# A graph layer without its column copies: VectorE's four copies a step go, GpSimd gathers eleven more times

## The chip, the cores and the metric

One Trainium2 chip, one NeuronCore of it. The kernel is one launch. The metric is device time in microseconds (us); lower is better. A core has five engines with queues of their own: TensorE (PE, matrix products into PSUM), VectorE (DVE), ScalarE (ACT), GpSimd (POOL) and SyncE (SP, here only a queue that issues DMAs). Transfers can be issued from SP, ACT and POOL.

## The reference

A message-passing layer over 12,500 nodes with 64 features and 200,000 edges that are sorted by destination. For every edge a gate is computed from its own 64 features and its distance, and a hidden state from its two end nodes; their product is added up at the destination, and a small network and a layer norm finish each node:

```python
nodes = node_state[edges].reshape(num_edges, -1)          # x[src], x[dst]
gates = ssp(edge_state @ We1 + be1) @ We2 + be2
gates = gates * (1.0 - sigmoid(5.0 * (edges_distance - 3.5)))
h = ssp(nodes @ Wn1 + bn1) @ Wn2 + bn2
message_sum = zeros.at[edges[:, 1]].add(h * gates)
new_state = node_state + (ssp(message_sum @ Ws1 + bs1) @ Ws2 + bs2)
out = layernorm(x + new_state)                            # ssp(x) = softplus(x) - log 2
```

Destinations are sorted, so their rows can be read as a window of a table. Sources are random: the 64 numbers of each of 200,000 source nodes have to be fetched one by one.

## The kernel before

**Groups and steps.** The edges are cut into 391 groups of 512, and a group into four slots k = 0 to 3 of 128 edges, one edge to a partition. The main loop (line 694) has one step i for each group. In the order in which each engine gets its instructions, step i does this:

- PE: `transposes(i+1)` (lines 346 to 356) turns the four slots of group i+1 from edges by features to features by edges; two bias products; `scatter(i-1)` (line 433), which adds the messages of group i-1 up by destination; `layer1_edge(i+1)` (line 370), `layer1_node(i+1)` (line 377), and the second layer of group i, `layer2` (lines 411 and 416).
- ACT: `xcopy(i+1)` (line 360) takes the transposed sources out of PSUM, then `exps` and `logs` (lines 391 and 394) make the softplus.
- DVE: `window(i-1)` (line 450) adds the scattered sums into the table of sums; `columns(i)` (lines 316 to 334); then `hcut(i)` (line 425), which waits for `layer2(i)` of PE, `message(i)` (line 429), `softplus(i+1)` (line 399) and `onehot(i+3)` (line 339).

A step of the loop closes through several engines: `hcut` lets `message` start, `message` lets PE's `scatter` start, `softplus` and `onehot` come before `window` on DVE, and PE's `layer1_edge` waits for `window`. In this document a step is counted from one `hcut` to the next.

**How a source row comes in.** There are three ways, and a slot is given to one of them beforehand:

1. Gathers. `gather(g)` (lines 245 to 257) issues one indirect DMA for a slot from POOL's queue: 128 rows of 256 bytes. The tiles of 18 groups (`AHEAD + BEHIND`) exist. The loop emits `gather(i+14)` in step i, but on POOL's own queue nothing holds it back except a free tile, and a tile is free when the scatter of the group 18 before it is done. So the gathers of group i+18 are issued as one burst right after `scatter(i)`.
2. Rows. Slots in `slots_by_rows` (47 of them) are fetched by plain DMAs of one row each, seven in a step from SP's queue and nine from ACT's (`fetch`, line 273).
3. Columns. Slots in `slots_by_columns` (line 119: slot 1 of the groups 42, 74, 106, ... 362, eleven in all). A copy of x, transposed, with nodes 0 to 6249 on partitions 0 to 63 and the rest on partitions 64 to 127, lies in SBUF as `xh`. In each of the steps 8 to 359 `columns(i)` loads four column numbers into registers of DVE (line 322) and copies four columns, each [128, 1] (line 329). After 32 steps the 128 columns of a slot are there, and one more operation (line 333) sets the half that belongs to the other node to zero. For such a slot no gather is issued, its part of the gather tile is set to zero (line 253), and `layer1_node` adds one more product on PE, `wn1_twice` by the chosen columns (line 380).

**Around the loop.** Before it, POOL issues the gathers of 14 groups back to back, and PE, ACT and DVE make the table of the nodes' own products (line 652) and write it out. `xh` comes in by four DMAs on SP's queue in steps 0 to 3 (line 700); the column numbers and the sides come in by two DMAs on SP's queue (lines 564 and 565), `wn1_twice` by two on ACT's (line 589), and three operations of DVE prepare them (lines 663 to 665). Nodes whose last edge is done go through the final network in blocks of 512, whose parts are spread over the following steps (`node_block`, lines 452 to 537); the last 512 nodes are two blocks of 256.

Of the kernel before, what the change touches and what calls it, by code (L numbers as in the profile page):

```python
# [42 lines left out]
F32 = mybir.dt.float32  # L43
BF16 = mybir.dt.bfloat16
I32 = mybir.dt.int32
U8 = mybir.dt.uint8
AF = mybir.ActivationFunctionType
OP = mybir.AluOpType
# [3 lines left out]
DVE = mybir.EngineType.DVE  # L52
# [5 lines left out]
P = 128  # L58
D = 64
# [6 lines left out]
K = 4  # L66
# [13 lines left out]
COLUMNS = 4  # L80
COLUMNS_FROM = 8
XH_PARTS = 4
# [34 lines left out]


def slots_by_columns(NG):

    slots = []
    for g in range(NG - 2):
        if (g - 3 - COLUMNS_FROM + 1) * COLUMNS >= (len(slots) + 1) * P:
            slots.append((g, 1))
    return slots


def column_columns(NG):

    return -(-len(slots_by_columns(NG)) // COLUMNS) * COLUMNS  # L130

# [8 lines left out]
def gnn_resnorm_kernel(ctx: ExitStack, tc: tile.TileContext, a: dict, out: bass.AP, E: int):  # L140
    nc = tc.nc
    x = a["x"]
    N = x.shape[0]
    NG = a["eT"].shape[1]
# [6 lines left out]
    REST = LOADS + 2  # L151
# [32 lines left out]
    packed, at = {}, 0  # L184
# [16 lines left out]
    half_n = a["xh"].shape[1]  # L201
    by_columns = {slot: n for n, slot in enumerate(slots_by_columns(NG))}
    columns_i = const.tile([P, column_columns(NG)], I32, name="columns_i")
    sides_i = const.tile([P, len(by_columns) * P], I32, name="sides_i")
    sides = sides_i.bitcast(F32)
    sign = const.tile([P, 1], F32, name="sign")
    border = const.tile([P, 1], F32, name="border")
    wn1_twice = const.tile([P, 2 * D], F32, name="wn1_twice")
# [33 lines left out]
    def padding(g, k):  # L242
        return g * GE + k % 2 * HE + k // 2 * P >= E

    def gather(g):

        xg = loads.tile([P, K, P], F32, name="xg", bufs=AHEAD + BEHIND)
        xgs[g] = xg
        for k in range(K):
            if (g, k) in by_rows:  # L250
                continue
            if padding(g, k) or (g, k) in by_columns:
                nc.vector.memset(xg[:, k, :D], 0.0)
                continue
            note(("gather", g), nc.gpsimd.indirect_dma_start(  # L255
                out=xg[:, k, :D], out_offset=None, in_=x,
                in_offset=bass.IndirectOffsetOnAxis(ap=src_i[:, g, k : k + 1], axis=0)))
# [56 lines left out]
    column_tiles, chosen_columns, columns_done = {}, {}, [0]  # L314

    def columns(i, pool):

        n = columns_done[0]
        if i < COLUMNS_FROM or n >= len(by_columns) * P:
            return  # L320
        p, q = (n // COLUMNS) % P, n // (COLUMNS * P) * COLUMNS
        _, at = nc.values_load_multi_w_load_instructions(  # L322
            columns_i[p : p + 1, q : q + COLUMNS], engines=[DVE], min_val=0, max_val=half_n - 1,
            skip_runtime_bounds_check_because="src holds rows of x")
        slot = list(by_columns)[n // P]
        if n % P == 0:
            column_tiles[slot] = pool.tile([P, P], F32, name="column", bufs=2)
        for j in range(COLUMNS):
            nc.vector.tensor_copy(column_tiles[slot][:, n % P + j : n % P + j + 1], xh[:, bass.ds(at[j], 1)])  # L329
        columns_done[0] += COLUMNS  # L330
        if columns_done[0] % P == 0:
            chosen_columns[slot] = pool.tile([P, P], F32, name="chosen", bufs=2)
            nc.vector.scalar_tensor_tensor(chosen_columns[slot], sides[:, n // P * P : (n // P + 1) * P], border,
                                           column_tiles[slot], OP.is_ge, OP.mult)

# [37 lines left out]
    def layer1_node(g):  # L373
        for h in range(2):
            zn = zs[g][:, h, HE * (1 - h) : HE * (2 - h)]
            chosen = [t for t in range(2) if (g, 2 * t + h) in by_columns]
            nc.tensor.matmul(zn, wns[:, g % REST, h, :], xTs[g][:, h], start=True, stop=not chosen,  # L377
                             skip_group_check=True)
            for t in chosen:
                nc.tensor.matmul(zn[:, t * P : (t + 1) * P], wn1_twice, chosen_columns[g, 2 * t + h], start=False,  # L380
                                 stop=True, skip_group_check=True)
# [162 lines left out]
    with tc.manual_schedule():  # L544
# [4 lines left out]
        with tc.tile_pool(name="prep", bufs=1) as prep:  # L549
# [14 lines left out]
            nc.sync.dma_start(columns_i, a["columns"])  # L564
            nc.sync.dma_start(sides_i, a["sides"].partition_broadcast(P))
# [21 lines left out]

            for h in range(2):
                nc.scalar.dma_start(wn1_twice[h * D : (h + 1) * D, :], a["Wn1"][:D, :])
                nc.vector.memset(sign[h * D : (h + 1) * D], 2.0 * h - 1.0)  # L590
                nc.vector.memset(border[h * D : (h + 1) * D], float(half_n if h else 1 - half_n))
# [55 lines left out]
            for i in range(PARTS):  # L647
# [10 lines left out]
                if i == 1:  # L658
                    nc.vector.tensor_copy(base_i[:1], base_b[:1])
                    nc.vector.tensor_scalar(base_i[32:33], base_b[32:33], float(8 * D), None, OP.mult)  # L660
                    nc.vector.tensor_scalar(rows_i, rows_i, float(4 * D), None, OP.mult)
                    upper = prep.tile([P, column_columns(NG)], F32, name="upper")
                    nc.vector.tensor_scalar(upper, columns_i, float(half_n), float(-half_n), OP.is_ge, OP.mult)
                    nc.vector.tensor_tensor(columns_i, columns_i, upper, OP.add)
                    nc.vector.tensor_scalar(sides, sides_i, sign, None, OP.mult)
                    for k in range(2):
                        nc.vector.tensor_copy(be3[:, k, :], rows[:, 0, :])
                    for k in range(K):
                        nc.vector.tensor_copy(row3[:, :, k, :], rows[:, 1:3, :])
                        nc.vector.tensor_copy(rs3[:, k, :], rows[:, 3, :])  # L670
# [9 lines left out]
        with tc.tile_pool(name="finish", bufs=1) as finish:  # L680
            xh = finish.tile([P, half_n], F32, name="xh")
# [12 lines left out]
            for i in range(-1, last - 1):  # L694
# [3 lines left out]
                if 0 <= i < XH_PARTS:  # L698
                    part = slice(half_n * i // XH_PARTS, half_n * (i + 1) // XH_PARTS)
                    nc.sync.dma_start(xh[:, part], a["xh"][:, part])  # L700
# [13 lines left out]
                columns(i, finish)  # L714
# [168 lines left out]
def layouts(inputs):  # L883
# [12 lines left out]
    def padded(v, n, fill):  # L896
        return np.concatenate([v, np.full((n - v.shape[0],) + v.shape[1:], fill, v.dtype)])
# [13 lines left out]
    chosen = np.concatenate([out["src_l"].reshape(P, NG, K)[:, g, k] for g, k in slots_by_columns(NG)])  # L911
    out["sides"] = np.ascontiguousarray(chosen)
    v = padded(chosen, P * column_columns(NG), 0).reshape(-1, P, COLUMNS)
    out["columns"] = np.ascontiguousarray(v.transpose(1, 0, 2).reshape(P, -1))
    half_n = -(-N // 2)
    out["xh"] = np.ascontiguousarray(np.concatenate([x[:half_n].T, padded(x[half_n:], half_n, 0.0).T]))
# [45 lines left out]
```

## Time and profile before

| | |
|---|---|
| median of 3 runs | 3303.51 us (3302.15 to 3305.52) |
| the profiled execution | 3302.15 us, with a span of 3300.4 us inside it |
| busy: PE, POOL, DVE, ACT | 2543.6, 1421.1, 1209.9, 968.5 us |
| granted TensorE clock, mean | 0.735 of full speed |
| gathers by POOL (line 255) | 1505, 944 ns each |
| row fetches: SP's queue, ACT's queue | 2688 and 3328 |
| column copies by DVE (line 329) | 1408, 153 ns each |

The first `hcut` is at 152.9 us and the last at 3286.4 us, so the 390 steps between them take 8.03 us each on average.

How such a profile is read: a line of the page's groups gives source line, engine and operation, the tiles it writes and reads, the count, then the busy time and the mean of one instruction, and after the bar the idle time of that engine just before these instructions with what ended most of it. A line of the timeline gives the start, the duration, the engine, the line and the operation; in brackets stands how long the engine was idle before and what ended it. "remote" means that the trace shows nothing that ended the wait. PE products are pipelined and their ends are modelled. The granted clock changes between 0.5 and 1.0 in this trace, and nothing in between.

### The profile page before, as it was taken

How to read it: one execution, taken by the hardware profiler on the slowest of the kernel's cores; microseconds unless marked ns; L12 is line 12 of the kernel's file. 1: busy time of each engine (PE TensorE's matmuls, PEld its weight loads, DVE VectorE, ACT ScalarE, POOL GpSimd, SP SyncE). 2: the span in 40 equal slices, each digit the busy share in tenths (PEclk: the TensorE clock that was granted, in tenths of full speed). 3: DMA queues.
4: the chain of work that ended last, by engine and by line, in shares of the span. 5: the costliest groups of instructions: out<-in, count | busy, mean ns of one | idle time of the engine just before them, and what ended most of it. 6: DMA issues, size and time to landing. Idle time of an engine off the chain costs nothing.

```text
span 3300.4 us, 50822 instructions
## 1 busy us (share of the span) xinstructions
PE 2543.6 (77%) x11400; PEld 2046.8 (62%) x11400; DVE 1209.9 (37%) x4216; ACT 968.5 (29%) x1323; POOL 1421.1 (43%) x1509
## 2 busy tenths in 40 slices
PE   1678788887777787878778877778877778777787
PEld 1566666666666666666666666666666666666565
DVE  1333333333333333333333333333333333333334
ACT  0232322232232232323233332323232233233333
POOL 7144444444444444444444444444444444444410
PEclk9976776676777667776777777777777676777767
DMA  5321111111111111111111111111111111111110
GB/s 144 120 53 39 41 39 39 37 40 38 44 39 40 40 38 43 39 46 38 43 39 40 41 40 43 42 41 41 37 45 41 41 42 41 41 42 41 42 34 14
DMA packets 152151, 147.35 MB, mean 45 GB/s; under 512 B 53023, under 2 KB 99147, under 8 KB 151842
## 3 DMA queue, kind: packets, MB, share of 16 engines
q1 hardware_dynamic: 95498, 92.19, 9.9%
q0 software_dynamic: 48160, 49.41, 7.7%
q10 hardware_dynamic: 8184, 2.44, 0.4%
q8 instruction: 96, 1.57, 0.2%
q14 instruction: 213, 1.74, 0.2%
HBM read 134.23 MB, written 9.63 MB: 44 GB/s over the span
## 4 chain that ended last, share of the span: by engine, by line
PE 59%; DVE 16%; issue 8%; another core or an unknown queue 8%; DVEq 7%; DMA 1%; SPq 0%; POOL 0%; ACT 0%; ACTq 0%; POOLq 0%
PE z L377 16%; PE gh L416 13%; PE z L370 11%; PE gh L411 8%; PE tx L353 5%; DVE h L425 4%; DVEq L441 4%; DVE s L399 4%; PE z L433 3%; DVEq L322 2%; DVE sums L450 2%; DVE xg L339 2%; DVE msg L429 2%; PE z L652 1%
## 5 line engine op out<-in xcount | busy, mean ns | idle before, releaser
L255 POOL DMA_INDIRECT xg<-in_x,src_i x1505 | 1420.9, 944 | 1740.8 <-PE z L433 564.5
L391 ACT ACTIVATE u<-z 128x768 f32<-128x768 f32 x392 | 316.9, 808 | 1706.0 <-issue 962.6
L425 DVE TENSOR_TENSOR h<-gh,cut 128x256 f32<-128x256 f32 x391 | 165.8, 424 | 1749.8 <-PE gh L416 854.3
L370 PE MATMUL z<-eT,consts 128*128 128x256 f32 x782 | 406.9, 617 | 378.3 <-DVE sums L450 309.8
L377 PE MATMUL z<-xT,wns 106*128 106x256 f32 x1564 | 657.7, 567 | 0.2 <-ACT xT L360 0.2
L416 PEld LDWEIGHTS gh<-consts,s 128*128 128x128 f32 x3128 | 540.3, 259 | 0.1
L416 PE MATMUL gh<-consts,s 128*128 128x64 f32 x3128 | 532.1, 330 | 0.0
L377 PEld LDWEIGHTS z<-xT,wns 106*128 106x128 f32 x1564 | 461.7, 295 | 112.0 <-ACT xT L360 0.9
L433 PE MATMUL z<-xg,msg 128*128 128x84 f32 x1556 | 313.2, 332 | 271.5 <-DVE msg L429 262.4
L433 PEld LDWEIGHTS z<-xg,msg 128*128 128x128 f32 x1556 | 245.1, 225 | 430.2 <-DVE msg L429 417.9
L370 PEld LDWEIGHTS z<-eT,consts 128*128 128x128 f32 x782 | 164.8, 263 | 447.2 <-DVE sums L450 371.3
L411 PEld LDWEIGHTS gh<-consts,s 128*128 128x128 f32 x1564 | 378.3, 298 | 56.8 <-DVE s L399 0.7
L394 ACT ACTIVATE u<-u,one 128x768 f32<-128x768 f32 x392 | 365.9, 933 | 69.7 <-issue 52.0
L399 DVE SCALAR_TENSOR_TENSOR s<-u,z 128x768 f32<-128x768 f32 x392 | 368.9, 941 | 10.7 <-ACT u L394 9.8
L411 PE MATMUL gh<-consts,s 128*128 128x128 f32 x1564 | 365.3, 380 | 0.4 <-DVE s L399 0.4
L360 ACT COPY xT<-tx 106x512 f32<-106x512 f32 x391 | 228.4, 584 | 414.0 <-PE tx L353 293.2
L353 PE MATMUL tx<-consts,xg 128*106 128x128 f32 x1517 | 282.2, 315 | 6.4 <-DMA wns<-table 6.4
L353 PEld LDWEIGHTS tx<-consts,xg 128*106 128x106 f32 x1517 | 222.3, 174 | 10.6 <-issue 8.0
L329 DVE COPY column<-xh 128x1 f32 x1408 | 174.2, 153 | 110.5 <-issue 104.7
L450 DVE TENSOR_TENSOR sums<-sums,z 64x42 f32 x778 | 150.7, 194 | 86.6 <-issue 38.2
L429 DVE TENSOR_TENSOR msg<-gh,h 128x256 f32<-128x256 f32 x391 | 165.8, 424 | 13.4
L404 PE MATMUL gh<-row,ones 3*128 3x512 bf16 x391 | 160.6, 411 | 0.0
(110 smaller groups left out, 756.6 us busy)
## 6 DMA issues: line engine op xcount, KB each, us to landing
xr<-in_x ACTq DMA_DIRECT2D x3328, 0.2 KB
eT<-in_eT SPq DMA_DIRECT2D x195, 256.0 KB
xr<-in_x SPq DMA_DIRECT2D x2688, 0.2 KB
xg<-in_x,src_i POOLq DMA_INDIRECT x1505
wns<-table SPq DMA_DIRECT2D x782, 21.0 KB
table<-tb SPq DMA_DIRECT2D x14, 448.0 KB
sums<-in_xT SPq DMA_DIRECT2D x7, 455.0 KB
y<-in_x SPq DMA_DIRECT2D x23, 128.0 KB
```

Of the source, the lines that this page charges most:

```text
L255: note(("gather", g), nc.gpsimd.indirect_dma_start(out=xg[:, k, :D], out_offset=None, in_=x, in_offset=bass.IndirectOffsetOnAxis(ap=src_i[ ...
L353: ins = nc.tensor.transpose(tx[:, k, :], xgs[g][:, k, :DW], ident)
L370: nc.tensor.matmul(zs[g][:, 0, :HE], we1.rearrange("a h d -> a (h d)"), eTs[g], start=False, stop=True, skip_group_check=True)
L377: nc.tensor.matmul(zn, wns[:, g % REST, h, :], xTs[g][:, h], start=True, stop=not chosen, skip_group_check=True)
L391: nc.scalar.activation(us[g][:, part], z_of(g)[:, part], AF.Exp)
L394: nc.scalar.activation(us[g][:, part], us[g][:, part], AF.Ln, bias=one)
L399: nc.vector.scalar_tensor_tensor(ss[g].rearrange("p i t e -> p (i t e)")[:, part], us[g][:, part], BIG, z_of(g)[:, part], OP.min, OP.max)
L411: nc.tensor.matmul(v[:, 0, t], ss[g][:, 0, t, :], we2, start=False, stop=False, skip_group_check=True)
L416: nc.tensor.matmul(ghs[g][:, 1, 2 * t + h, :], ss[g][:, 1 + h, t, :], wn2, start=False, stop=h == 1 and t == 1, skip_group_check=True)
L425: nc.vector.tensor_mul(hs[g], ghs[g][:, 1], cut[:, g, :].to_broadcast([P, K, D]))
L429: nc.vector.tensor_mul(msgs[g], ghs[g][:, 0], hs[g])
L433: ins = nc.tensor.matmul(sc, msgs[g][:, 2 * t : 2 * t + 2, :].rearrange("p h f -> p (h f)"), xgs[g][:, 2 * t : 2 * t + 2, D:DW], start=t = ...
```

## The change

The column copies and all that serves them are taken out: `slots_by_columns`, `columns`, `xh` with its four loads, the two loads of numbers and sides, the two loads of `wn1_twice`, the memsets of `sign` and `border`, the three preparing operations, the extra product of `layer1_node`, and the arrays made for them on the host. The eleven slots that came by columns are gathered by POOL like any other: 1516 gathers in place of 1505, and no zeroing of their tiles. Nothing else moves: rows, loads, node blocks and the order of the loop stay as they are.

```diff
@@ slots
-def slots_by_columns(NG):
-    slots = []
-    for g in range(NG - 2):
-        if (g - 3 - COLUMNS_FROM + 1) * COLUMNS >= (len(slots) + 1) * P:
-            slots.append((g, 1))
-    return slots
@@ gather
-            if padding(g, k) or (g, k) in by_columns:
+            if padding(g, k):
                 nc.vector.memset(xg[:, k, :D], 0.0)
                 continue
@@ columns
-    def columns(i, pool):
...
-        _, at = nc.values_load_multi_w_load_instructions(
-            columns_i[p : p + 1, q : q + COLUMNS], engines=[DVE], min_val=0, max_val=half_n - 1,
...
-        for j in range(COLUMNS):
-            nc.vector.tensor_copy(column_tiles[slot][:, n % P + j : n % P + j + 1], xh[:, bass.ds(at[j], 1)])
...
-            nc.vector.scalar_tensor_tensor(chosen_columns[slot], sides[:, n // P * P : (n // P + 1) * P], border,
-                                           column_tiles[slot], OP.is_ge, OP.mult)
@@ layer1_node
-            chosen = [t for t in range(2) if (g, 2 * t + h) in by_columns]
-            nc.tensor.matmul(zn, wns[:, g % REST, h, :], xTs[g][:, h], start=True, stop=not chosen,
+            nc.tensor.matmul(zn, wns[:, g % REST, h, :], xTs[g][:, h], start=True, stop=True,
                              skip_group_check=True)
-            for t in chosen:
-                nc.tensor.matmul(zn[:, t * P : (t + 1) * P], wn1_twice, chosen_columns[g, 2 * t + h], start=False,
-                                 stop=True, skip_group_check=True)
@@ before the loop
-            nc.sync.dma_start(columns_i, a["columns"])
-            nc.sync.dma_start(sides_i, a["sides"].partition_broadcast(P))
...
-            for h in range(2):
-                nc.scalar.dma_start(wn1_twice[h * D : (h + 1) * D, :], a["Wn1"][:D, :])
-                nc.vector.memset(sign[h * D : (h + 1) * D], 2.0 * h - 1.0)
-                nc.vector.memset(border[h * D : (h + 1) * D], float(half_n if h else 1 - half_n))
...
-                    nc.vector.tensor_scalar(upper, columns_i, float(half_n), float(-half_n), OP.is_ge, OP.mult)
-                    nc.vector.tensor_tensor(columns_i, columns_i, upper, OP.add)
-                    nc.vector.tensor_scalar(sides, sides_i, sign, None, OP.mult)
@@ the loop
-                if 0 <= i < XH_PARTS:
-                    part = slice(half_n * i // XH_PARTS, half_n * (i + 1) // XH_PARTS)
-                    nc.sync.dma_start(xh[:, part], a["xh"][:, part])
...
-                columns(i, finish)
```

More of the change, by code (lines that the diff above doesn't have):

```diff
@@ L79 @@
 LANDED = 4
-COLUMNS = 4
-COLUMNS_FROM = 8
-XH_PARTS = 4
 CUTOFF = 5.0
@@ L116, in slots_by_rows @@
     return slots
-def slots_by_columns(NG):
-    slots = []
-    for g in range(NG - 2):
-        if (g - 3 - COLUMNS_FROM + 1) * COLUMNS >= (len(slots) + 1) * P:
-            slots.append((g, 1))
-    return slots
-def column_columns(NG):
-    return -(-len(slots_by_columns(NG)) // COLUMNS) * COLUMNS
 def row_columns(NG):
@@ L200, in gnn_resnorm_kernel @@
     rs3 = const.tile([PIECES, K, D], BF16, name="rs3")
[L201 to L208, printed above, removed]
     wns = const.tile([DW, REST, 2, 2 * D], F32, name="wns")
@@ L312, in load @@
                 table_bytes[:, bass.ds(bases[g][h], 8 * D * W)].rearrange("o (w f) -> (o w) f", w=W))), old)
-    column_tiles, chosen_columns, columns_done = {}, {}, [0]
-    def columns(i, pool):
[L318 to L321, printed above, removed]
-        _, at = nc.values_load_multi_w_load_instructions(
-            columns_i[p : p + 1, q : q + COLUMNS], engines=[DVE], min_val=0, max_val=half_n - 1,
[L324 to L327, printed above, removed]
-        for j in range(COLUMNS):
[L329 to L332, printed above, removed]
-            nc.vector.scalar_tensor_tensor(chosen_columns[slot], sides[:, n // P * P : (n // P + 1) * P], border,
-                                           column_tiles[slot], OP.is_ge, OP.mult)
     xTs, zs, us, ss, ghs, hs, msgs, scs = ({} for _ in range(8))
@@ L661, in gnn_resnorm_kernel @@
                     nc.vector.tensor_scalar(rows_i, rows_i, float(4 * D), None, OP.mult)
-                    upper = prep.tile([P, column_columns(NG)], F32, name="upper")
-                    nc.vector.tensor_scalar(upper, columns_i, float(half_n), float(-half_n), OP.is_ge, OP.mult)
-                    nc.vector.tensor_tensor(columns_i, columns_i, upper, OP.add)
-                    nc.vector.tensor_scalar(sides, sides_i, sign, None, OP.mult)
                     for k in range(2):
@@ L680, in gnn_resnorm_kernel @@
         with tc.tile_pool(name="finish", bufs=1) as finish:
-            xh = finish.tile([P, half_n], F32, name="xh")
             blocks = list(zip(node_blocks(N), block_steps(N, NG)))
@@ L910, in layouts @@
     out["rows"] = np.ascontiguousarray(np.concatenate(rows, axis=1))
[L911 to L916, printed above, removed]
     out["dst_l"] = lanes(dst, dst[-1])
```

## The prediction

> **What bounds the kernel now.** I read the page's groups first, then the chain of waits, then the timeline of single steps. By the page POOL looks harmless and DVE's copies look free:
>
> ```profile
> span 3300.4 us, 50822 instructions
> L255 POOL DMA_INDIRECT xg<-in_x,src_i x1505 | 1420.9, 944 | 1740.8 <-PE z L433 564.5
> L425 DVE TENSOR_TENSOR h<-gh,cut 128x256 f32<-128x256 f32 x391 | 165.8, 424 | 1749.8 <-PE gh L416 854.3
> L329 DVE COPY column<-xh 128x1 f32 x1408 | 174.2, 153 | 110.5 <-issue 104.7
> ```
>
> POOL is idle for 1740.8 us, waiting for scatters to free tiles, and it works 17 to 18 groups ahead of PE. DVE idles 1749.8 us in front of `hcut` (4.5 us a step), and the copies lie inside that time. The chain names PE's products. The timeline of a step whose PE work ran at full clock tells something else:
>
> ```profile
> 253.95 0.68 PE L433 MATMUL z<-xg,msg 128*128 128x84 f32 x4
> 254.90 0.94 POOL L255 DMA_INDIRECT xg<-in_x,src_i  x1 [3.05 <-PE z L433]
> 255.38 0.50 DVE L329 COPY column<-xh 128x1 f32 x4
> 256.14 0.94 POOL L255 DMA_INDIRECT xg<-in_x,src_i  x1 [0.30 <-issue]
> 257.22 1.00 PE L416 MATMUL gh<-consts,s 128*128 128x64 f32 x8
> 257.39 0.95 POOL L255 DMA_INDIRECT xg<-in_x,src_i  x1 [0.30 <-issue]
> 258.64 0.94 POOL L255 DMA_INDIRECT xg<-in_x,src_i  x1 [0.31 <-issue]
> 260.75 0.42 DVE L425 TENSOR_TENSOR h<-gh,cut 128x256 f32<-128x256 f32 x1 [4.87 <-remote]
> 260.81 0.58 ACT L360 COPY xT<-tx 106x512 f32<-106x512 f32 x1 [1.93 <-remote]
> ```
>
> PE's last product of `layer2` ends at 258.22, but `hcut`, which needs nothing else, starts at 260.75, and ACT's `xcopy` 0.06 us behind it. Both start 1.2 us after the last gather of the burst ended (259.58), which is when its data land: in the packet records of the gather queue the last landing of a burst lies 1.17 to 1.19 us, on average, behind its last gather. Here is a step whose burst has three gathers, because slot 1 of group 202 comes by columns:
>
> ```profile
> 1624.81 0.67 PE L433 MATMUL z<-xg,msg 128*128 128x84 f32 x4 [0.66 <-DVE msg L429]
> 1625.75 0.94 POOL L255 DMA_INDIRECT xg<-in_x,src_i  x1 [3.03 <-DVE s L399]
> 1627.00 0.94 POOL L255 DMA_INDIRECT xg<-in_x,src_i  x1 [0.30 <-issue]
> 1628.08 1.00 PE L416 MATMUL gh<-consts,s 128*128 128x64 f32 x8
> 1628.24 0.94 POOL L255 DMA_INDIRECT xg<-in_x,src_i  x1 [0.30 <-issue]
> 1630.12 0.42 DVE L425 TENSOR_TENSOR h<-gh,cut 128x256 f32<-128x256 f32 x1 [3.39 <-PE tx L353]
> ```
>
> Again `hcut` comes 0.94 us after the last gather, but that one ended 1.25 us sooner, and the step took 6.25 us. After the last gather of all, PE alone decides:
>
> ```profile
> 3237.46 1.00 PE L416 MATMUL gh<-consts,s 128*128 128x64 f32 x8
> 3238.50 0.42 DVE L425 TENSOR_TENSOR h<-gh,cut 128x256 f32<-128x256 f32 x1 [2.94 <-PE gh L416]
> ```
>
> So something that PE signals to DVE and ACT is held until a burst has landed. Why a transfer that is needed 15 steps later holds them, the trace does not show; that it does, it shows all over. I went through steps 0 to 371 by the starts of `hcut`, the scatters and the gathers. A burst starts 0.27 us after its scatter and 1.88 us after `hcut` at the earliest; four gathers take 4.69 us from first start to last end, three 3.44. Of 317 steps with four gathers 255 have the next `hcut` within 1.35 us of the burst's end; of 52 with three only 20. The floor of a step with four gathers is 1.88 + 4.69 + 1.17 = 7.74 us, and 7.7 to 7.8 is the commonest step. Between steps 8 and 359 a step with four gathers takes 8.18 us on average (299), with three 7.45 (49): 0.73 less.
>
> **The change part by part.**
>
> *Eleven more gathers.* Each of the eleven slots sits in a burst of three that becomes one of four: 1.25 us later (0.94 and an issue of 0.30). What the step pays is 1.25 + 1.17 less the distance that `hcut` has now from the burst's end, and nothing where that is over 2.42. In the steps that start at 342.5, 596.9, 853.3, 1112.9, 1369.5, 1623.9, 1880.6, 2140.4, 2404.0, 2667.7 and 2930.2 us the distances are 1.51, 2.21, 2.67, 1.06, 1.45, 0.94, 2.04, 1.94, 3.52, 0.96 and 1.07. The price is 0.91, 0.21, 0, 1.36, 0.97, 1.48, 0.38, 0.48, 0, 1.46 and 1.35: **+8.6 us**. The average gives 11 x 0.73 = 8.0. Ends: 0, if the burst holds nothing, and 11 x 1.25 = 13.8. POOL itself has the time, and the data are needed 15 steps later.
>
> *The product with `wn1_twice` goes* (line 380; 0.43 us in the chain at half clock, so about 0.22 at full). It lies on PE between `layer1_node` and `layer2`, on the way to `hcut`, in eleven steps. In eight of them `hcut` stands 1.01 to 1.26 us behind a burst, so the landing covers it. In the other three (735.1, 2807.1, 3067.3 us) it gives 0.22 to 0.43: **-0.65 us** at the full-clock price of all three, ends 0 and 11 x 0.43 = -4.7.
>
> *The preparation.* DVE's three operations stand in front of the copy that frees PE's buffer: `sides` starts at 107.99, and PE resumes at 110.37.
>
> ```profile
> 107.99 0.95 DVE L665 TENSOR_SCALAR sides_i<-sides_i,sign 128x1408 f32<-128x1408 int32 x1
> 110.37 5.84 PEld L652 LDWEIGHTS z<-consts,sums 65*128 65x128 f32 x27 [1.74 <-DVE tb L655]
> ```
>
> They go from 107.70 to 108.86, and PE's products run one behind the other from there to the end of the table: **-1.15 us**, ends 0 and -1.2. The five small and large loads ahead of that on SP's and ACT's queues (704, 6 and twice 32 KB, and their places among the transfers' semaphores) give nothing: the x parts behind them were in by 43 us, while PE and ACT stood still until 104.3 us in a stretch full of gathers that stay. I keep 10 us either way for that stretch.
>
> *The column work in the loop.* Per step one register load, four address operations and four copies, 0.5 us, start 0.06 us after the sums, and `hcut` waits 4 us more: 0, and the cover is PE's half of the step (5.2 us on average), which at its shortest, 2.94 us at full clock, still covers the 1 us. The zeroing (11 x 0.11 us) and the selection (11 x 0.35) lie in the same shadow. `xh`'s four loads (781 KB) on SP's queue, past the loads and rows of steps 0 to 3: the bursts there land 1.1 us after their end like the others, so 0.
>
> The sum is 8.6 - 0.65 - 1.15 = +6.8 us on the profiled execution's 3302.15, which is 1.4 below the median. On the median: 3303.51 + 6.8 = **3310.3**, said as 3310.5. That is +0.21%, and about 0.2% (6.6 us) is what a measurement of this kernel can tell from no change.
>
> [...] The gathers in the stretch with copies (206 to 3047 us) take 943 ns each, those without (3055 to 3140 us) 943 ns as well, and the last landing of a burst comes 1.17 to 1.19 us behind its end with the copies and 1.17 without. [...]
>
> **The rivals.**
>
> 1. *The copies make the hold longer; faster.* A single mechanism at the end of the burst: with the copies `hcut` stands 1.176 us behind it (mean of 234 landing-bound steps), without them 1.11 (11 steps at both ends of the loop). If the copies are the cause, 255 x 0.066 = 17 us come back: 3310.3 - 17 = 3293. It passes zero at 0.027 us a step and 0.2% faster at 0.053. For it: the steps at 177.9 and 198.4 us, just before the copies start, took 6.33 and 6.23 us at full clock with four gathers, where all 47 like them with copies took 7.66 to 8.0. Against it: the ones at 3051.8 and 3109.8 us, without copies, took 7.78 and 7.70, and the landings themselves are no sooner.
> 2. *POOL's burst is only a bystander*, as its idle time says and as its lead of 17 groups suggests. Then the gathers cost 0 and the rest stands: 3303.5 - 1.8 = 3301.7, no change. Against it: 0.73 us between steps of three and four gathers.
> 3. *The longer bursts cost more than themselves.* While PE waits for a landing its clock falls (0.5 in most of PE's halves, 0.74 overall), and a step that follows may lose its full clock. If each of the eleven pays the whole 1.25 us and the step behind it the 0.44 us by which the average (8.18) stands over the floor (7.74), it is 11 x 1.69 - 1.8 = +16.8 us: 3320. Against it: the step after one with three gathers takes 8.17 us now, no less than the others.
>
> **How the numbers follow.** The gathers' price as summed 0.64, rival 1 0.17, rival 2 0.09, rival 3 0.10. Inside the first the terms spread by some 4 us, and its middle lies on the 0.2% mark, so it is slower by over 0.2% in 0.40 and within 0.2% in 0.24; its own range is 3304 to 3317. Rival 1 counts 0.15 as faster and 0.02 as the same, rival 2 as the same, 0.02 of it as faster for the stretch before the loop; rival 3 as slower. That is 0.17 faster, 0.33 the same, 0.50 slower. The range reaches to rival 1 on one side and to the upper end of the gathers' price (13.8 - 1.2 + 3303.5 = 3316) and a part of rival 3 on the other: 3291 to 3320.
>
> **What will show it.** Right: 1516 gathers; the eleven steps named above have four gathers, and `hcut` again 1.1 to 1.3 us behind the last one; steps of four gathers elsewhere still about 8.18 us; the first `hcut` about 1 us earlier. Wrong: full-clock steps with four gathers of 6 to 6.5 us throughout the loop (rival 1); the eleven steps unchanged in length (rival 2); a mean clock well below 0.73 (rival 3); a first `hcut` moved by many us.

## The result, and the profile after

The kernel after takes 3215.77 us (median of 4 runs, 3204.55 to 3235.73), the kernel before 3304.52 us in the same comparison: a ratio of 0.9737, with a 95% interval of 0.9688 to 0.9786. It is 2.6% faster; the forecast was 3310.5 us, slower by 0.2%. Two later comparisons on other chips gave 0.9763 (0.9698 to 0.9827) and 0.9769 (0.9725 to 0.9812).

From the page of the kernel after (span, gathers, `hcut`; the columns of a group are those explained above):

```profile
span 3202.7 us, 47723 instructions
...
L230 POOL DMA_INDIRECT xg<-in_x,src_i x1516 | 1431.8, 944 | 1638.2 <-DVE s L348 549.5
...
L374 DVE TENSOR_TENSOR h<-gh,cut 128x256 f32<-128x256 f32 x391 | 166.0, 424 | 1936.3 <-PE gh L365 1022.1
```

The gathers are eleven more and last 944 ns, as before. In front of `hcut` DVE now idles 1936.3 us. Before, the idle time there, the copies and the idle time in front of the copies made 1749.8 + 174.2 + 110.5 = 2034.5 us. The copies did lie inside DVE's wait, as the prediction said; but the wait itself has become 98.2 us shorter, which is as much as the spans differ (97.7).

Almost all of it lies in the loop: the first `hcut` comes at 150.5 us in place of 152.9, and the 390 steps take 7.792 us each in place of 8.035, which is 94.7 us. In the timeline the difference looks like this. These are two neighbouring full-clock steps of the kernel after, each with four gathers (the first two gathers of a burst, and most of PE and ACT, are left out):

```profile
366.94 1.00 PE L365 MATMUL gh<-consts,s 128*128 128x64 f32 x8
367.12 0.94 POOL L230 DMA_INDIRECT xg<-in_x,src_i  x1 [0.30 <-issue]
367.18 3.74 SPq L256 DMA_DIRECT2D xr<-in_x  x7
...
368.37 0.94 POOL L230 DMA_INDIRECT xg<-in_x,src_i  x1 [0.30 <-issue]
...
368.94 0.42 DVE L374 TENSOR_TENSOR h<-gh,cut 128x256 f32<-128x256 f32 x1 [3.91 <-PE tx L306]
...
370.44 0.59 ACT L313 COPY xT<-tx 106x512 f32<-106x512 f32 x1 [1.84 <-remote]
...
373.15 1.00 PE L365 MATMUL gh<-consts,s 128*128 128x64 f32 x8
373.33 0.94 POOL L230 DMA_INDIRECT xg<-in_x,src_i  x1 [0.31 <-issue]
...
374.58 0.94 POOL L230 DMA_INDIRECT xg<-in_x,src_i  x1 [0.30 <-issue]
...
376.80 0.42 DVE L374 TENSOR_TENSOR h<-gh,cut 128x256 f32<-128x256 f32 x1 [5.55 <-remote]
376.86 0.59 ACT L313 COPY xT<-tx 106x512 f32<-106x512 f32 x1 [2.06 <-remote]
```

In both steps PE's last product for `hcut` ends within the third gather (367.94 and 374.15). In the first, `hcut` starts 0.88 us after the end of the third gather, while the fourth is still at work, and only `xcopy` is held, to 1.13 us after the fourth: the step takes 6.2 us. In the second both are held to the landing of the fourth, and the step takes 7.9 us. So a held signal goes out at one of the landings (the packets of that third gather end from 368.89 to 369.24 us), and which one it catches is open from step to step. In the kernel after 32 of the 185 starts of `hcut` that come 0.25 us late or more lie 0.8 to 1.1 us behind the end of a gather that another one follows; before it was 1 of 193.

I counted the holds over steps 8 to 358: the steps in which PE's last product for `hcut` ended at least 0.3 us ahead of the landing of the burst's last gather (taken as 1.18 us after its end), and how many of them started `hcut` within 0.25 us of that landing. Before it was 186 of 193, after it is 136 of 195. Of the steps with a burst of four gathers that ran at full clock from one `hcut` to the next, none of 27 took less than 6.6 us before, and 15 of 41 do after. Added up over all steps, `hcut` starts after PE's last product by 270 us before and by 206 us after (beyond 0.05 us; in a step that is not held it starts 0.04 us after): 64 of the 94.7 us. The other 31 were not taken apart: PE itself is busy for 2483 us in the loop before and for 2441 after, at a mean granted clock of 0.723 and 0.733, and why the clock differs no run shows.

One of the eleven steps that got a fourth gather, which took 6.25 us before, isn't held at all: the third gather of its burst is under way and the fourth still to come when `hcut` starts 0.04 us after PE's end, 5.24 us after the one ahead of it.

```profile
1570.34 0.42 DVE L374 TENSOR_TENSOR h<-gh,cut 128x256 f32<-128x256 f32 x1 [5.47 <-PE gh L365]
...
1574.54 1.00 PE L365 MATMUL gh<-consts,s 128*128 128x64 f32 x8
...
1574.95 0.94 POOL L230 DMA_INDIRECT xg<-in_x,src_i  x1 [0.30 <-issue]
1574.96 0.59 SPq L256 DMA_DIRECT2D xr<-in_x  x2
...
1575.58 0.42 DVE L374 TENSOR_TENSOR h<-gh,cut 128x256 f32<-128x256 f32 x1 [2.94 <-issue]
```

### The profile page after: what moved, and what is told of

Read it like the earlier page. It is cut to its first block, busy times and chain, and to the rows that moved or that the text cites. A ratio compares the mean times of both kernels' runs of the same rounds, so it can differ in the third digit from the quotient of the medians.

```text
span 3202.7 us, 47723 instructions
## 1 busy us (share of the span) xinstructions
PE 2498.8 (78%) x11378; PEld 2007.8 (63%) x11378; DVE 1031.8 (32%) x2779; ACT 969.4 (30%) x1323; POOL 1432.0 (45%) x1520
## 4 chain that ended last, share of the span: by engine, by line
PE 63%; DVE 17%; issue 10%; another core or an unknown queue 5%; DVEq 4%; DMA 1%; ACT 0%; ACTq 0%; POOL 0%; SPq 0%
PE z L329 17%; PE gh L365 13%; PE z L323 12%; PE gh L360 8%; PE tx L306 5%; DVE h L374 4%; PE z L382 4%; DVE sums L399 4%; DVE s L348 3%; DVEq L390 3%; DVE xg L292 2%; DVE msg L378 1%; PE gh L353 1%; PE z L594 1%
## 5 line engine op out<-in xcount | busy, mean ns | idle before, releaser
L374 DVE TENSOR_TENSOR h<-gh,cut 128x256 f32<-128x256 f32 x391 | 166.0, 424 | 1936.3 <-PE gh L365 1022.1
L323 PE MATMUL z<-eT,consts 128*128 128x256 f32 x782 | 395.8, 601 | 388.9 <-DVE sums L399 325.4
L329 PE MATMUL z<-xT,wns 106*128 106x256 f32 x1564 | 643.7, 557 | 1.2 <-ACT xT L313 1.2
L365 PEld LDWEIGHTS gh<-consts,s 128*128 128x128 f32 x3128 | 533.8, 257 | 0.1
L329 PEld LDWEIGHTS z<-xT,wns 106*128 106x128 f32 x1564 | 449.7, 288 | 108.2 <-ACT xT L313 1.6
L382 PE MATMUL z<-xg,msg 128*128 128x84 f32 x1556 | 306.5, 327 | 208.9 <-DVE msg L378 167.7
L360 PEld LDWEIGHTS gh<-consts,s 128*128 128x128 f32 x1564 | 373.2, 293 | 56.2 <-DVE s L348 0.2
L292 DVE TENSOR_TENSOR xg<-consts,rel 128x168 f32<-128x168 f32 x391 | 127.3, 326 | 0.0
```

What stands on the lines that cost most here:

```text
L323: nc.tensor.matmul(zs[g][:, 0, :HE], we1.rearrange("a h d -> a (h d)"), eTs[g], start=False, stop=True, skip_group_check=True)
L360: nc.tensor.matmul(v[:, 0, t], ss[g][:, 0, t, :], we2, start=False, stop=False, skip_group_check=True)
L365: nc.tensor.matmul(ghs[g][:, 1, 2 * t + h, :], ss[g][:, 1 + h, t, :], wn2, start=False, stop=h == 1 and t == 1, skip_group_check=True)
L374: nc.vector.tensor_mul(hs[g], ghs[g][:, 1], cut[:, g, :].to_broadcast([P, K, D]))
L382: ins = nc.tensor.matmul(sc, msgs[g][:, 2 * t : 2 * t + 2, :].rearrange("p h f -> p (h f)"), xgs[g][:, 2 * t : 2 * t + 2, D:DW], start=t = ...
```

## The experiments

The theory is rival 1 made stronger: DVE's column work doesn't lengthen every hold by a little, it makes the hold last to the whole burst's landing. Its rivals: the gain comes from the preparation or the loads of `xh`; or from the data that the copies move; or from the clock alone. Chips differ (the kernel before took 2677 us on one and 3295 on another), so that a time stands beside that of the kernel before or after on the same chip.

### Which part of the column work

Three kernels made from the kernel before. The first drops the copies:

```diff
             column_tiles[slot] = pool.tile([P, P], F32, name="column", bufs=2)
-        for j in range(COLUMNS):
-            nc.vector.tensor_copy(column_tiles[slot][:, n % P + j : n % P + j + 1], xh[:, bass.ds(at[j], 1)])
+            nc.vector.memset(column_tiles[slot], 0.0)
```

> The kernel before without the four column copies of a step (the tile they fill is zeroed once per slot, so the eleven slots count as zero); the register load, its address operations, the loads of xh, the preparation, line 380 and the 1505 gathers stay. If the copies themselves hold PE's signal until the whole burst has landed, the time falls to 3200 to 3215 us, and full-clock steps with four gathers of 6.2 to 6.3 us appear by the dozen. If the register load does it, the time stays at 3300 to 3306 us, with none of them between steps 8 and 359.

The second drops the register load and takes fixed columns:

```diff
-        _, at = nc.values_load_multi_w_load_instructions(columns_i[...], engines=[DVE], ...)
-            nc.vector.tensor_copy(column_tiles[slot][:, n % P + j : n % P + j + 1], xh[:, bass.ds(at[j], 1)])
+            nc.vector.tensor_copy(column_tiles[slot][:, n % P + j : n % P + j + 1], xh[:, n + j : n + j + 1])
```

> The kernel before with its four copies a step, but from columns whose places are known when the kernel is built (the wrong ones, so the eleven slots hold other nodes' data): no register load and no address operation on DVE. If the copies do it, it stays at 3300 to 3306 us; if the register load does, it falls to 3200 to 3215 us; if both have a share, it lies between.

The third drops both and keeps what stands ahead of the loop (its eleven slots count as zero); the fourth kernel of this comparison is the kernel after with its eleven slots zeroed in place of gathered (`if padding(g, k) or (g, k) in zeroed:`).

> The kernel before with neither register load nor copies in the loop (the eleven slots count as zero); the loads of xh, columns, sides and the doubled weights, the preparation, line 380 and the 1505 gathers stay. If the gain comes from DVE's work in the loop, this has all of it and saves the eleven gathers besides: 3200 to 3212 us. If it comes from what was loaded or prepared, 3295 to 3306 us.

> The kernel after with the eleven slots zeroed instead of gathered, 1505 gathers as before. By the prediction's price of 0.2 to 1.5 us a gather it is 8.6 us below the kernel after: 3207 us. If a longer burst costs nothing, 3216; if each costs more than itself, 3200 us or below.

Measured, with the kernel before at 3295.0 us (3278 to 3310) on that chip: 3238.8 (3213 to 3242) without copies, 3254.3 (3245 to 3276) with four fixed copies, 3213.6 (3198 to 3242) with neither, 3204.1 (3192 to 3220) for the kernel after without the eleven gathers. Held to the last landing, by the count above: 141 of 195, 165 of 198, 134 of 193 and 139 of 196.

The set-up is no cause: the third kernel keeps all of it and has the whole gain, 81 us. In its profile the holds to the last landing are as few as in the kernel after, but `hcut` is late by 235 us in all, not 206, and PE's busy time in the loop is shorter, 2415 us against 2441, at a granted clock of 0.744 against 0.733; so how the gain divides between hold and clock isn't the same in every execution. The copies alone, with fixed places, cost 41 us of it and bring back a good part of the holds. The first kernel did not test what it was meant to: with nothing to use the registers, the built program has no register load left, only one wait of DVE per step in its place (352 instructions), and its range overlaps that of the third. The rest, 41 us between four fixed copies and the kernel before, belongs to the load, the four address operations and the copies' computed places together. The fourth kernel's ratio, 0.9724 (0.9664 to 0.9784), is not to be told from the 0.9737 of the kernel after, so these runs do not resolve the price of eleven gathers.

### With and without the row fetches

The next four take out row fetches. The cut is the same in each; `keep` names the queue that is left:

```diff
-    slots = slots_by_rows(NG)
+    slots = [slot for slot in slots_by_rows(NG) if slot[0] in keep]
+    dropped = {(g, k) for queue, g, k in slots_by_rows(NG) if queue not in keep}
...
-            if padding(g, k):
+            if (g, k) in dropped or padding(g, k):
```

> The kernel after without the row fetches of SP and ACT in the loop (6016 small transfers; the 47 slots they fill are zeroed by DVE and count as zero); the 1516 gathers stay. In a stretch of the profile after, the third gather's landing lets hcut go and the fourth's lets xcopy go, while SP's row issues beside them take 0.7 us each. If the hold comes from these issues meeting a burst, the 206 us by which hcut starts after PE's last product go: 3010 us or below. If the gathers alone hold PE's signals, nothing changes: 3205 to 3220 us.

> The same cut in the kernel before (47 slots zeroed, no row fetches; register loads, copies and everything else stay). If DVE's column work costs time only by making the hold longer, and the hold comes from the row fetches, it is within 10 us of the run above. If the column work costs time of its own, or the hold is the gathers' alone, it stays 70 to 95 us above it.

> The kernel after without SP's row fetches alone (2688; 21 slots zeroed). If SP's issues beside the burst make the hold, about 3010 us, as without any rows; if ACT's make it, 3205 to 3220 us.

> The kernel after without ACT's row fetches alone (3328; 26 slots zeroed). At the loop's end, where ACT's have run out and SP's have not, two of the last steps with four gathers were not held at all: if ACT's issues make the hold, about 3010 us; if SP's do, 3205 to 3220 us.

These ran on another chip, which behaves differently: the kernel before took 2676.6 us there (2655 to 2688) at a clock of 0.83 to 0.84. Measured: 2535.4 us without any rows, 2589.3 for the kernel before without rows, 2608.1 without SP's, 2599.2 without ACT's; as ratios to the kernel before 0.947, 0.967, 0.973 and 0.969. None of the four has a hold: `hcut` starts 0.04 us after PE's last product in every kind of step. So they do not say who makes the hold on the other chips, and the expectations above can't be judged by their times. They do show one thing: with the column work the kernel without rows still takes 54 us more at the median, with no hold at all. From the pages of the two kernels without rows, first made from before, then from after (spans, and the groups of `hcut`):

```profile
span 2584.0 us, 37761 instructions
...
L426 DVE TENSOR_TENSOR h<-gh,cut 128x256 f32<-128x256 f32 x391 | 166.0, 424 | 1185.2 <-PE gh L417 1185.2
```

```profile
span 2556.8 us, 34607 instructions
...
L375 DVE TENSOR_TENSOR h<-gh,cut 128x256 f32<-128x256 f32 x391 | 166.0, 425 | 1434.6 <-PE gh L366 1434.6
```

PE's product is all that releases `hcut` in both; the clocks of these two runs are 0.851 and 0.859. A full-clock step has a median of 5.25 us in both; what differs is how much of the time runs at full clock. The single runs of the two lie on one line of time against clock (2563 us at 0.860 with the column work, 2559 at 0.859 without). So here its cost goes with the granted clock: 0.847 to 0.860 with it, 0.859 to 0.872 without. Why the clock is lower with it, no run shows.

### Number, time or data

All of these are made from the kernel after, by lines put behind `window` in steps 8 to 359, where `columns` stood; `spare` is a tile of 128x512 that nothing else uses. Twelve narrow copies, then one wide one:

```diff
                 at(window, i - 1)
+                if 8 <= i < 360:
+                    for j in range(12):
+                        nc.vector.tensor_copy(spare[:, j : j + 1], consts[:, j : j + 1])
```

```diff
+                    nc.vector.tensor_copy(spare, consts[:, :512])
```

> The kernel after once more, so that the three others can be compared with it on one chip: the chip of the last four runs ran the kernel before in 2677 us with hcut never held, the chip ahead of it in 3295. Expected: 0.97 to 0.98 of the kernel before on either.

> The kernel after with twelve copies of one column (128x1, fixed places, consts to a spare tile) in each of steps 8 to 359, where the kernel before had four. Four fixed copies cost 41 us (3254 against 3214). If the cost goes with the number of DVE's instructions, twelve cost 100 to 125 us, 3 to 4% over the kernel after on the same chip; if DVE's work beside a burst merely tips it into the longer hold and that is saturated, 40 to 80 us, and nothing on a chip without the hold.

> The kernel after with one copy of 128x512 a step in that place, about as long as four copies of one column, with 128 times their data. If the number of instructions counts, a quarter of the four copies' cost, 10 us; if the time in which DVE is busy counts, 30 to 45 us; if the amount of data moved counts, 100 us or more, by the granted clock. If such copies keep POOL from working, the gathers beside them take longer than 943 ns.

Measured on one chip: the kernel after 3183.2 us (3168 to 3196), twelve narrow copies 3280.0 (3270 to 3297), one wide copy 3183.1 (3180 to 3192). Held: 131 of 212, 185 of 199, 150 of 213. The wide copy is as long as the four copies of the kernel before were (0.43 us against 0.5), moves 128 times their data and costs nothing; twelve narrow copies bring the kernel back to the time of the kernel before (3269.0 us on that chip). Their 97 us lie between the two forecasts, 100 to 125 by number and 40 to 80 for a hold that is saturated. So neither DVE's busy time nor the amount of data decides. The first fence is the wide copy itself (shortest, median and longest in ns, then first and last start), the second the gathers of its kernel, the third those of the kernel after on that chip:

```profile
L650 DVE COPY spare<-consts x352: 426/427/678, 205.1 to 2947.9; 128x512 f32<-128x512 f32 x176
```

```profile
L230 POOL DMA_INDIRECT xg<-in_x,src_i x1516 | 1443.9, 952 | 1611.8 <-DVE s L348 519.1 <-PE z L382 441.0 <-issue 362.6
```

```profile
L230 POOL DMA_INDIRECT xg<-in_x,src_i x1516 | 1434.6, 946 | 1601.4 <-DVE s L348 537.3 <-PE z L382 497.5 <-issue 362.2
```

The gathers that overlap a wide copy take 968 ns, the others 945; those that overlap the narrow ones 945 and 945. So a gather beside a wide copy took 23 ns longer and one beside the narrow copies no longer, and neither cost time in that way: with the wide copies the kernel took 3183.1 us, without them 3183.2.

The same data as the wide copy in four instructions, and narrow copies on ACT instead of DVE:

```diff
+                    for j in range(4):
+                        nc.vector.tensor_copy(spare[:, j * P : (j + 1) * P], consts[:, j * P : (j + 1) * P])
```

```diff
+                    for j in range(8):
+                        nc.scalar.copy(spare[:, j : j + 1], consts[:, j : j + 1])
```

> The kernel after with four copies of 128x128 on DVE in each of steps 8 to 359: the data of the one copy of 128x512, which cost nothing, in as many instructions as the kernel before had copies. If the number of instructions counts, 30 to 50 us over the kernel after (0.985 to 0.992 of the kernel before, where the kernel after stood at 0.974 and 0.976); if only narrow copies or register addresses count, nothing (0.97 to 0.98).

> The kernel after with eight copies of one column (128x1) on ACT in each of steps 8 to 359, between its third early row fetch and its exponentials, where it is idle for some 3 us, beside the same part of the burst. If any engine's instructions beside a burst lengthen the hold, 50 to 80 us over the kernel after (0.99 to 1.0 of the kernel before); if it is DVE's alone, nothing (0.97 to 0.98).

Measured, with the kernel before at 3296.8 us: 3239.0 (3233 to 3253), a ratio of 0.982 (0.977 to 0.986), and 3290.1 (3281 to 3302), 0.998 (0.995 to 1.001). With the kernel after at 0.976 of the kernel before, 3217 us, they cost 22 and 73 us. Held: 152 of 193 and 173 of 195. That the four instructions cost something where one cost nothing is not shown: their interval meets those of the kernel after on other chips (0.970 to 0.983 and 0.973 to 0.981). The eight copies on ACT are clear of them, and cost about as much for each as the narrow ones on DVE, so it is not a matter of DVE alone. ACT's copies lay in its idle time; after the last of the eight it stays idle for 2.4 us in the median step:

```profile
L651 ACT COPY spare<-consts x2816: 185/187/193, 209.0 to 3042.7; 128x1 f32<-128x1 f32 x188
```

The last step takes the data away altogether: twelve empty instructions on DVE, in the place where the twelve narrow copies cost 97 us.

```diff
+                    for j in range(12):
+                        nc.vector.engine_nop()
```

> [...] If what counts is that an instruction is issued and retired, 60 to 100 us over the kernel after, 0.99 to 1.005 of the kernel before; if it is the copies' reads and writes, nothing, 0.97 to 0.98.

> The kernel after as the reference of the run above: 0.97 to 0.98 of the kernel before.

Measured on one chip: 3301.2 us (3285 to 3315) with the empty instructions, 3218.1 (3211 to 3225) without: 83 us, and the kernel is back at 1.001 (0.998 to 1.004) of the kernel before. By the trace the twelve are through in 0.16 us in the median step. The line of the empty instructions (count, then shortest, median and longest duration in ns):

```profile
L650 DVEq ENGINE_NOP  x4224: 5/8/14, 209.0 to 3048.1; - x192
```

A full-clock step of this kernel, in the timeline:

```profile
361.69 1.00 PE L365 MATMUL gh<-consts,s 128*128 128x64 f32 x8
361.86 0.95 POOL L230 DMA_INDIRECT xg<-in_x,src_i  x1 [0.30 <-issue]
...
363.11 0.94 POOL L230 DMA_INDIRECT xg<-in_x,src_i  x1 [0.31 <-issue]
...
365.22 0.42 DVE L374 TENSOR_TENSOR h<-gh,cut 128x256 f32<-128x256 f32 x1 [5.44 <-remote]
365.28 0.58 ACT L313 COPY xT<-tx 106x512 f32<-106x512 f32 x1 [1.66 <-remote]
```

PE's products end 0.1 us ahead of the third gather's end, as in the two steps shown of the kernel after, and both signals come with the fourth landing. Of 193 steps 186 are held, exactly the count of the kernel before. The table of the loop, first with the empty instructions, then without (stretch, length, busy time and number of instructions of PE, PEld, DVE, ACT and POOL, clock, DMA):

```profile
151.90:3274.70 3122.80, 2471.92 (x11128) 1984.76 (x11126) 990.42 (x2682) 948.20 (x1291) 1362.78 (x1444) 0.72 0.18 40
```

```profile
149.60:3203.20 3053.60, 2465.30 (x11128) 1976.90 (x11125) 991.74 (x2682) 949.59 (x1292) 1363.02 (x1444) 0.72 0.18 41
```

The loops differ by 69 us at the same clock (0.724 in both, with one digit more) and with nearly the same busy time of every engine (PE's differs by 7 us). `hcut` is late by 278 us in the one and by 213 in the other: 65 of the 69 are the hold.

### A kernel without row fetches, on chips with the hold

The kernel after with the 47 slots of the rows gathered by POOL too (the cut of the row fetches above, with nothing zeroed), and the same with twelve narrow copies. It computes everything.

> The kernel after with no row fetches at all and the 47 slots gathered by POOL (1563 gathers). Without the fetches and without the 47 slots the ratio to the kernel before was 0.947 on the chip without the hold. If 47 gathers cost 0.2 to 1.5 us each, 0.95 to 0.97, faster than the kernel after; if POOL becomes the bound, 0.98 or above.

> The kernel after with no row fetches and 1563 gathers once more, as the reference of the next run on its chip: 0.87 to 0.89 of the kernel before.

> The same with twelve copies of one column a step on DVE in steps 8 to 359, which cost the kernel after 97 us. If DVE's instructions cost time only through the hold that the row fetches bring about, 0 to 10 us here; if they also lower the granted clock by themselves (without the row fetches, on the chip without a hold, the column work still cost 40 to 54 us at a clock lower by 0.014), 40 us or more.

Measured on two chips: 2877.3 us, 0.879 (0.872 to 0.885) of the kernel before, and 2864.7 us, 0.861 (0.856 to 0.867). That is a tenth less than the kernel after (3183.2 us on the first of the two chips), and less than was expected. With the twelve copies it is 2920.7 us (2911 to 2928) on the second chip: 56 us above the median of the four runs without them, which spread from 2831 to 2883 us, and 79 us above their two quickest, on which the ratio 0.861 rests. Without the row fetches the page reads

```profile
span 2875.2 us, 35003 instructions
...
L231 POOL DMA_INDIRECT xg<-in_x,src_i x1563 | 1479.2, 946 | 1268.6 <-PE z L383 470.7
...
L375 DVE TENSOR_TENSOR h<-gh,cut 128x256 f32<-128x256 f32 x391 | 166.1, 425 | 1597.3 <-issue 927.4
```

and a full-clock step with its fourth gather still to come

```profile
1243.61 1.00 PE L366 MATMUL gh<-consts,s 128*128 128x64 f32 x8
1244.04 0.94 POOL L231 DMA_INDIRECT xg<-in_x,src_i  x1 [0.30 <-issue]
...
1244.65 0.42 DVE L375 TENSOR_TENSOR h<-gh,cut 128x256 f32<-128x256 f32 x1 [2.94 <-issue]
...
1245.09 0.59 ACT L314 COPY xT<-tx 106x512 f32<-106x512 f32 x1
```

Here `hcut` starts 0.04 us after PE, in the middle of a burst. Of 305 steps one is held; with the twelve copies 17 of 289 are held to the last landing and 54 more are late by less, and `hcut`'s lateness goes from 8 to 53 us. (On the first chip, without the copies, it was 3 of 312 and 20 us.) So gathers alone hardly make a hold, and some of it comes back with added instructions where there are no row fetches. The row fetches are the most of the instructions that went, with their register moves and loads: 47723 - 35003 = 12720. But they are 6016 transfers as well, and no run here tells whether they feed the hold by their number or by their transfers. Nor are the 306 us all hold: on the first chip `hcut`'s lateness falls from 189 to 20 us, and the granted clock is 0.791 in place of 0.752.

### What an instruction costs

Put on one scale, each cost over the number of instructions added: the change itself 88.8 us for 50822 - 47723 = 3099, 29 ns; four fixed copies 41 us for 1397 (against the kernel with the set-up alone), 29 ns; twelve narrow copies 97 for 4224, 23; eight on ACT 73 for 2816, 26; four of 128x128 22 for 1408, 16; twelve empty ones 83 for 4224, 20; the row fetches 306 us (3183.2 less 2877.3 on one chip) for 12720, 24, with what their transfers cost. The four of 128x128 are not clear of the noise. Twelve copies where the hold is nearly gone cost 13 to 19 ns each, and one wide copy nothing that could be measured (352 instructions would be 10 us by this scale, which the runs do not exclude).

## Why the prediction was wrong

**The step that failed** is the column work in the loop, "0, and the cover is PE's half of the step". The cover held: the copies, and later the empty instructions, lay wholly in DVE's idle time. What failed is the idea that an instruction in idle time costs only its duration. Nine instructions a step (a register load, four address operations, four copies) let nearly every hold run to the last landing (186 of 193), and without them 3 in 10 end sooner (59 of 195). In place of 0 the term was about -90 us.

**Rival 1** named the right place and the right sign, and its mark, full-clock steps of 6 to 6.5 us throughout the loop, is what the profile after shows. Its price, 17 us, was mis-sized, since it took the distance of `hcut` from the burst's end over steps that were bound by the landing. A mean over held steps can't show that steps stop being held. The number that would have told it stood beside it: no step of 47 with copies released early, two of four without them. By that, half of the 47 full-clock steps, at some 1.5 us each, would have come to 35 us, and the steps at mixed clock to more. The two held steps at the end of the loop were taken as evidence against the rival; where some holds end early and others don't (59 and 136 of 195 in the kernel after) they are none.

**The eleven gathers**, +8.6 us: the eleven steps took 81.6 us together before and 85.3 after, so +3.7, with two of them released early, at 5.25 and 6.26 us. The kernel without these gathers is not told from the kernel after, so neither the sign nor the size of the term is settled by the runs. Steps with four gathers still take longer than those with three (7.91 and 7.25 us), which is against rival 2.

**The small terms.** The first `hcut` came 2.4 us sooner (-1.15 was summed), but between kernels that are the same up to there it varies from 146.8 to 151.9 us, so that says little. The set-up with `xh`'s loads costs nothing that shows, as summed. For line 380's product no run was made alone, and the prediction priced it in steps that lie one too late: the product at 730.96 us belongs to the step that ends with the `hcut` at 735.1, not to the one that starts there. In the right steps `hcut` comes within 1.35 us of the burst's end in six of eleven, and the other five would have given 1.1 to 2.2 us, not 0.65. (In the same way the held step of 7.70 us near the loop's end starts at 3102.1, and 3109.8 is its end.)

**Rival 3**, a falling clock, went the other way: the mean clock rose from 0.735 to 0.744.

**The gathers beside the copies** last no longer than the others, as the prediction read in the trace of the kernel before: 943 ns with the copies and without. The wide copies show a small effect, 23 ns (968 against 945 ns) on each gather that overlaps one, far below the 0.43 us of the copy, and the narrow ones none (945 and 945).

**What stays open** is why the number of added instructions bears on when PE's signal comes through (twelve copies a step cost 97 us, twelve empty instructions 83, one wide copy nothing that shows), why chips differ in it, and why the clock is lower with the column work where there is no hold. Fetching the instructions is not the direct cause: of the 193 steps counted in the kernel before, 73 have no packet of either instruction queue in them, and 70 of these were held. Semaphores that the added instructions raise are not it either: of the twelve narrow copies only the last one raises one, and the empty instructions, which cost 83 us, raise none. The recording of the profile is a candidate that was not tested: every run here has a span and a granted clock, so none was free of it, and no run can show what it costs.

## What to carry to other kernels

Work in an engine's idle time isn't free because it is covered: where a signal between two other engines comes late for no reason that the trace names, count the instructions issued per step on all engines: here, on the chips with the hold and with the recording on, small added instructions came to 13 to 29 ns each whatever they did; on the chip without the hold no signal came late. One wide copy was better than twelve narrow ones (3183.1 us against 3280.0), and a gather of 128 rows in one instruction better than 128 fetches of one row (2877.3 us against 3183.2, for 47 slots). To judge a hold, count how many steps are held and how many are not; the mean length of those that are held can't show that some cease to be.

## What was not expected of the hardware

- Twelve empty instructions of 8 ns on DVE, 0.16 us in all, cost 0.24 us a step; eight narrow copies on idle ACT cost 0.21.
- PE's signals to DVE and to ACT came at different landings of one burst: 368.94 and 370.44 us in the step shown.
- The same kernel takes 2677 us on one chip, with no hold and a clock of 0.83 to 0.84, and 3269 to 3305 on the others, at 0.72 to 0.75. Its first `hcut` came there at 84 to 86 us in the four kernels profiled, against 147 to 153 on the others, so the set-up is 61 us or more shorter there too.
- Some 6000 fetches of single rows, which were to spare POOL 47 gathers, cost over 300 us; gathering those 47 slots instead brought the kernel to 2865 and 2877 us.
